# Opening of a four-layer graph network kernel: zero products while x arrives, a different order of x W, and nine small loads issued later

## The chip, the cores and the metric

One core of a Trainium2 chip. The metric is the device time of one execution in microseconds (us). Every kernel is timed in several rounds beside the kernel before, on the same chip; I quote the median of its runs and, in brackets, the lowest and the highest. One run of each kernel was recorded by the hardware profiler. Its "span", from first to last instruction, is some 1.8 us shorter than the timed figure of the same execution.

Engines: PE is TensorE (PEld its weight loads), DVE is VectorE, ACT is ScalarE, SP is SyncE. "ACTq" marks the issue of a load by ScalarE.

## The reference, cut to what matters

x is 4096 x 128, adj is 4096 x 4096 in fp32 (67 MB), read again by every layer. Each layer is followed by a residual and a layer norm. Only the first layer matters here:

```python
def _L0_gnn_ref(h, node_adj, edge_adj, W, a):        # both adjacencies are adj
    hw = h @ W
    pos = (node_adj > 0); neg = (node_adj < 0)
    h_plus = pos @ hw;    h_minus = neg @ hw
    a1, a2 = a[:F_OUT], a[F_OUT:]
    e_plus  = leaky_relu((h_plus @ a1 + h_minus @ a2)[:, 0], ALPHA)
    e_minus = ...
    scores = where(edge_adj > 0, e_plus[None, :], NEG_INF)
    scores = where(edge_adj < 0, e_minus[None, :], scores)
    attn = softmax(scores, axis=1)
    return attn * edge_adj @ hw
# [...] layers 1 to 3: Chebyshev convolution, four-head attention, GraphSAGE mean
```

The kernel uses that adj holds no negative entry (it checks this, and has another path if it fails). Then `h_plus @ a1` is `pos @ (h @ (W a1))`. So two columns u = x (W a) per node are enough for e, and x W with u appended is one product of 130 columns.

## The kernel before

adj arrives in blocks of 512 x 512 (1 MB each), eight for each of eight rounds. ScalarE issues the loads of x^T (eight pieces) and, right behind them, nine loads of small tensors that only later layers use:

```python
    for g in range(NB):
        nc.scalar.dma_start(xT[:, g * IB:(g + 1) * IB], xT_in[:, g * IB:(g + 1) * IB])
    B1A = load_const(b1a, [P, HH], "B1A")
    # [...] B1B, W2, ATS, ATD, B2R: loaded by ScalarE in the same way
    nc.scalar.dma_start(W2S[:, 0:F], w2T)
    nc.scalar.dma_start(W3[:, 0, :], w3n)
    nc.scalar.dma_start(W3[:, 1, :], w3s)

    def later_constants(psum, name):                # "the setup work"
        # [...] 8 small copies from ATS and ATD into att; a product of W2 and att
        nc.vector.tensor_tensor(W3[:, 1, :], W3[:, 1, :], ident, ALU.add)      # L118
        # [...] the mean of W3 by a product, subtracted from W3
```

The opening of the first layer, x W for 32 tiles of 128 nodes, then rounds over the blocks:

```python
            for g in range(NB):
                tb = slice(g * TB, (g + 1) * TB)
                for half in range(2):
                    # [...] pn <- two products of an x tile with WA = [W, W a]      (TensorE)
                    nc.vector.tensor_copy(u[:, two, :], pn[:, :, F:F + 2])        # L320
                    nc.scalar.copy(hw[:, two, :], pn[:, :, 0:F])                  # L321
                split3(both[:, tb, :], 0, u[:, tb, 0])      # u as three bf16 parts: 5 VectorE ops per 4 tiles
            later_constants(ps_mm, "pmm")

            for i in range(NB):                        # rounds
                # [...] for each of 8 blocks: pos = mask(a) on VectorE, sums of u over it on TensorE,
                #       a scan for negative entries on ScalarE, products of known blocks with hw
                parts = l0w.tile([P, IB], F32, name="parts")
                nc.scalar.copy(parts, pe)
                sums = columns(parts)                  # the round's column sums, L340
                # [...] e, exp(e), and hw scaled by it, on VectorE and ScalarE
```

The framework that builds the kernel orders each engine's instructions by itself. An instruction whose inputs look ready can move forward past others, unless it is pinned (`keep_in_program_order`) or depends on late data.

Of the kernel before, what the change touches and what calls it, by code (L numbers as in the profile page):

```python
# [11 lines left out]
F32 = mybir.dt.float32  # L12
BF16 = mybir.dt.bfloat16
I32 = mybir.dt.int32
AF = mybir.ActivationFunctionType
ALU = mybir.AluOpType
# [3 lines left out]
P = 128  # L20
IB = 512
TB = IB // P
# [11 lines left out]
def adj_resnorm_d4(ctx: ExitStack, tc: tile.TileContext, x_in, xT_in, adj, adjT, w0g, w0gT, a0, w1a, b1a,  # L34
# [7 lines left out]
    nc = tc.nc  # L42
# [13 lines left out]
    def load_const(src, shape, name):  # L56
        t = const.tile(shape, F32, name=name)
        nc.scalar.dma_start(t, src)
        return t
# [5 lines left out]
    W0 = load_const(w0g, [P, F], "W0")  # L65
    for g in range(NB):
        nc.scalar.dma_start(xT[:, g * IB:(g + 1) * IB], xT_in[:, g * IB:(g + 1) * IB])
    B1A = load_const(b1a, [P, HH], "B1A")
    B1B = load_const(b1b, [P, 1], "B1B")
    W2 = load_const(w2, [P, F], "W2")  # L70
    ATS = load_const(att_src.rearrange("o h f -> (h f) o"), [P, 1], "ATS")
    ATD = load_const(att_dst.rearrange("o h f -> (h f) o"), [P, 1], "ATD")
    B2R = load_const(b2.to_broadcast([P, F]), [P, F], "B2R")

    W2S = const.tile([P, F + H], F32, name="W2S")
    nc.scalar.dma_start(W2S[:, 0:F], w2T)
    W3 = const.tile([P, 2, F], F32, name="W3")
    nc.scalar.dma_start(W3[:, 0, :], w3n)
    nc.scalar.dma_start(W3[:, 1, :], w3s)

    ident = const.tile([P, P], F32, name="ident")
    make_identity(nc, ident)
# [10 lines left out]
    WD = const.tile([P, 96], F32, name="WD")  # L93
    selD = const.tile([96, H, P], BF16, name="selD")

    def later_constants(psum, name):

        with tc.tile_pool(name="setup", bufs=1) as pool:
            att = pool.tile([P, 2, H], F32, name="att")
            nc.vector.memset(att, 0.0)  # L100
            for h in range(H):
                hp = slice(h * FO, (h + 1) * FO)
                nc.vector.tensor_copy(att[hp, 0, h:h + 1], ATS[hp, :])
                nc.vector.tensor_copy(att[hp, 1, h:h + 1], ATD[hp, :])

            nc.vector.memset(WD, 0.0)
            pw = psum.tile([P, 2, H], F32, name=name)
            nc.tensor.matmul(pw, W2, att.rearrange("p s h -> p (s h)"), start=True, stop=True)
            nc.vector.tensor_copy(W2S[:, F:F + H], pw[:, 0, :])
            for part in range(3):  # L110
                nc.vector.tensor_copy(WD[:, 32 * part:32 * part + H], pw[:, 1, :])

            rows = pool.tile([96, H], F32, name="rows")
            nc.vector.tensor_reduce(rows, ident[0:96, :].rearrange("p (q c) -> p c q", q=4)[:, 0:H, 0:3], AX.X, ALU.add)
            nc.vector.tensor_copy(selD, rows[:, :, None].to_broadcast([96, H, P]))


            nc.vector.tensor_tensor(W3[:, 1, :], W3[:, 1, :], ident, ALU.add)  # L118
            mean = pool.tile([P, P], F32, name="mean")
            nc.vector.memset(mean, 1.0 / F)  # L120
            pw = psum.tile([P, 2 * F], F32, name=name)
            nc.tensor.matmul(pw, mean, W3.rearrange("p s f -> p (s f)"), start=True, stop=True)
            nc.vector.tensor_sub(W3.rearrange("p s f -> p (s f)"), W3.rearrange("p s f -> p (s f)"), pw)

    def chunk(pool, src, ib, c, name="chunk"):

        t = pool.tile([P, TB, IB], F32, name=name)
        nc.sync.dma_start(t, src[ib, c])
        return t
# [133 lines left out]
    def layer0(ld, ps_acc, ps_tr, ps_mm):  # L263
# [9 lines left out]
        with tc.tile_pool(name="l0", bufs=1) as l0, tc.tile_pool(name="l0w", bufs=2) as l0w, \  # L273
# [25 lines left out]
            def split3(dst, col, v):  # L299

                for part in range(3):
                    nc.vector.tensor_copy(dst[:, :, col + part], v)
                    if part < 2:
                        nc.vector.tensor_sub(v, v, dst[:, :, col + part])


            WA = l0.tile([P, F + 2], F32, name="WA")
            pw = ps_mm.tile([P, 2], F32, name="pmm")
            nc.tensor.matmul(pw, W0T, A0, start=True, stop=True)
            nc.vector.tensor_copy(WA[:, 0:F], W0)  # L310
            nc.vector.tensor_copy(WA[:, F:F + 2], pw)
            for g in range(NB):
                tb = slice(g * TB, (g + 1) * TB)
                for half in range(2):
                    two = slice(g * TB + 2 * half, g * TB + 2 * half + 2)
                    pn = ps_mm.tile([P, 2, F + 2], F32, name="pmm")
                    for k in range(2):
                        t = g * TB + 2 * half + k
                        nc.tensor.matmul(pn[:, k, :], xT[:, t * P:(t + 1) * P], WA, start=True, stop=True)
                    nc.vector.tensor_copy(u[:, two, :], pn[:, :, F:F + 2])  # L320
                    nc.scalar.copy(hw[:, two, :], pn[:, :, 0:F])  # L321
                split3(both[:, tb, :], 0, u[:, tb, 0])
            later_constants(ps_mm, "pmm")

            def masks(a):
                pos = l0w.tile([P, TB, IB], BF16, name="pos", bufs=4)
                nc.vector.tensor_scalar(pos, a, 0.0, None, op0=ALU.is_gt)
                return pos

            def edge_sums(pe, pos, j, wgt, first, last):  # L330

# [11 lines left out]
            def product(p, j, a, first, last):  # L343
                for k in range(TB):
                    nc.tensor.matmul(p, hw[:, j * TB + k, :], a[:, k, :], start=first and k == 0,  # L345
                                     stop=last and k == TB - 1)
# [24 lines left out]
            for i in range(NB):  # L371
# [6 lines left out]
                for n, j in enumerate(order):  # L378
                    if i < j <= i + 2:
                        a = chunk(l0k, adjT, i, j, f"keep{j - i}")  # L380
                        kept[i].append((j, a))
                    else:
                        a = chunk(ld, adjT, i, j)
                    own = a
                    pos = masks(a)
                    edge_sums(pe, pos, j, both, n == 0, n == NB - 1)
                    junk = l0w.tile([P, TB, IB], BF16, name="junk", bufs=1)
                    nc.scalar.activation(junk, a, AF.Relu, scale=-1.0, accum_out=bad[:, i * NB + n:i * NB + n + 1])
                    if n == 1 and rest:
                        diagonal(*rest)  # L390
                        if i >= 3:
                            above(i - 3, kept.pop(i - 3))
                    if j <= i and p is None and n > 0:
                        p = ps_acc.tile([P, IB], F32, name="pacc")
                    if j < i:
                        known.append((j, a))
                    while n > 0 and known:
                        j, a = known.pop(0)
                        product(p, j, a, j == 0, False)
                if i == 4:  # L400
                    tc.keep_in_program_order(nc.sync.dma_start(x, x_in.rearrange("(t p) f -> p t f", p=P)))
                parts = l0w.tile([P, IB], F32, name="parts")
                nc.scalar.copy(parts, pe)
# [621 lines left out]
```

## Time and profile before

| | kernel before |
|---|---|
| time before the prediction | 2262.8 us (2258.33 to 2266.13, 3 runs) |
| the execution that was profiled | 2259.04 us, span 2257.2 us |
| TensorE busy | 2134.4 us, 95% of the span |
| from 90 us on | TensorE nearly full |
| column sums of rounds 0, 1, 2 | 47.04, 65.53, 90.16 us |
| first product of the second layer | 348.0 us |

I use the last two rows as milestones throughout: they tell how far the kernel has come without waiting for the end.

A line of a timeline gives start, duration, engine, source line, operation, output and input with shapes; in brackets how long the engine stood idle before it and what ended that.

### The profile page before, as it was taken

The page shows a single profiled execution, that of the slowest core. Times are in us where ns is not written, and L with a number is a line of the kernel's source. Part 1 is how long each engine was busy: PE and PEld are TensorE (multiplying, and loading weights), DVE is VectorE, ACT ScalarE, POOL GpSimd, SP SyncE. Part 2 cuts the span into 40 slices and gives each one's busy share as a digit, 9 for nine tenths or more (in the row PEclk, how much of TensorE's full clock was granted, in tenths as well). Part 3 has the DMA queues.
Part 4 walks back from the last instruction along what each step waited for, and adds up shares of the span by engine and source line. Part 5 has one row for each costly group of instructions (what it writes and reads, how often), then busy time and mean ns, then how long its engine had stood idle before and what let it go on. Part 6 is the DMA issues. An engine that isn't in the chain of part 4 may idle for free. (4 is left out here: it accounts for less than half of the span.)

```text
span 2257.2 us, 22860 instructions
## 1 busy us (share of the span) xinstructions
PE 2134.4 (95%) x8560; PEld 847.2 (38%) x8560; DVE 1174.2 (52%) x1828; ACT 565.6 (25%) x1032; POOL 853.8 (38%) x539
## 2 busy tenths in 40 slices
PE   5899999999999999999999999968999899999997
PEld 3333444444444444444443333312222222323334
DVE  5544462000011100000025777779999999999995
ACT  5765200000000000000032322334343433332213
POOL 0000000000000000000004667679999899989990
PEclk8899999999999999999999999989999999999999
DMA  8886658888776676778766556614666566545545
GB/s 315 339 322 223 224 170 275 300 302 301 267 260 240 228 267 237 264 272 278 265 238 225 205 205 223 220 58 152 230 239 241 205 228 251 214 146 205 184 171 169
DMA packets 87144, 528.17 MB, mean 234 GB/s; under 512 B 9328, under 2 KB 15472, under 8 KB 25712
## 3 DMA queue, kind: packets, MB, share of 16 engines
q1 hardware_dynamic: 78992, 521.31, 65.6%
q10 hardware_dynamic: 8032, 5.31, 0.7%
q8 instruction: 69, 1.13, 0.2%
q14 instruction: 51, 0.42, 0.1%
HBM read 524.49 MB, written 2.10 MB: 233 GB/s over the span
## 5 line engine op out<-in xcount | busy, mean ns | idle before, releaser
L715 DVE SCALAR_TENSOR_TENSOR tau<-D,es,a 128x1024 f32<-128x1024 f32 (+1 forms) x640 | 646.3, 1058 | 60.2 <-ACT a L687 33.8
L721 POOL TENSOR_TENSOR tau<-tau,chunk 128x1024 f32<-128x1024 f32 x192 | 455.8, 2374 | 14.4 <-DVE tau L715 13.7
L621 POOL TENSOR_TENSOR x<-x,B2R 128x512 f32<-128x512 f32 x8 | 10.2, 1274 | 1172.6 <-PE px L135 1172.6
L737 PE MATMUL num<-tau,hc 128*32 128x512 f32 x2048 | 324.5, 615 | 12.9 <-POOL tau L721 6.0
L737 PE MATMUL den<-tau,cs 128*32 128x512 f32 x2048 | 331.5, 603 | 4.4 <-DVE tau L715 3.0
L813 PE MATMUL pp<-chunk,xT 128*128 128x512 f32 (+1 forms) x488 | 231.6, 604 | 0.9 <-ACT D L703 0.9
L687 ACT ACTIVATE a<-chunk 128x1024 f32<-128x1024 f32 x160 | 164.3, 1027 | 246.1 <-DVE tau L719 209.1
L513 PE MATMUL pacc<-chunk,t 128*128 128x512 f32 x512 | 223.5, 592 | 0.0
L513 PE MATMUL pacc<-chunk,v 128*128 128x512 f32 x512 | 222.5, 592 | 0.0
L513 PE MATMUL pacc<-chunk,x 128*128 128x512 f32 x512 | 221.9, 592 | 0.0
L720 POOL TENSOR_TENSOR tau<-tau,chunk 128x320 f32<-128x320 f32 x192 | 167.0, 870 | 140.4 <-DVE tau L715 78.7
L937 PE MATMUL pp<-chunk,w 128*128 128x512 f32 x448 | 203.6, 598 | 1.5 <-DVE oT L597 0.8
L345 PE MATMUL pacc<-chunk,hw 128*128 128x512 f32 x408 | 196.1, 621 | 2.3 <-DVE hw L410 2.3
L719 DVE TENSOR_TENSOR tau<-tau,a 128x704 f32<-128x704 f32 x192 | 168.5, 877 | 0.0
L727 POOL TENSOR_TENSOR tau<-tau,chunk 128x1024 f32<-128x1024 f32 x64 | 151.8, 2372 | 1.1
L737 PEld LDWEIGHTS den<-tau,cs 128*32 128x32 f32 x2048 | 78.9, 111 | 179.5 <-issue 102.8
L513 PEld LDWEIGHTS pacc<-chunk,v 128*128 128x128 f32 x512 | 97.2, 190 | 122.0 <-issue 122.0
L737 PEld LDWEIGHTS num<-tau,hc 128*32 128x32 f32 x2048 | 60.6, 110 | 218.5 <-issue 115.6
L513 PEld LDWEIGHTS pacc<-chunk,x 128*128 128x128 f32 x512 | 96.4, 190 | 116.7 <-issue 116.7
L513 PEld LDWEIGHTS pacc<-chunk,t 128*128 128x128 f32 x512 | 96.1, 190 | 115.3 <-issue 115.3
L813 PEld LDWEIGHTS pp<-chunk,xT 128*128 128x128 f32 x488 | 85.7, 189 | 130.3 <-issue 127.6
L560 DVE COPY w<-ptr 128x512 f32<-128x512 f32 x8 | 5.5, 691 | 241.5 <-PE ptr L135 241.5
(212 smaller groups left out, 1665.4 us busy)
## 6 DMA issues: line engine op xcount, KB each, us to landing
chunk<-in_adjT SPq DMA_DIRECT2D x386, 1024.0 KB, 4.8
chunk<-in_adj SPq DMA_DIRECT2D x80, 1024.0 KB, 5.0
chunk<-in_adj SPq DMA_DIRECT2D x32, 512.0 KB, 4.8
keep<-in_adjT SPq DMA_DIRECT2D x13, 1024.0 KB, 7.2
xT<-in_xT ACTq DMA_DIRECT2D x8, 256.0 KB, 6.2
out<-o ACTq DMA_DIRECT2D x7, 256.0 KB, 2.3
W1A<-in_w1a ACTq DMA_DIRECT2D x1, 384.0 KB, 5.9
W1B<-in_w1b ACTq DMA_DIRECT2D x1, 384.0 KB, 6.7
```

The lines of the kernel that those rows point to most:

```text
L345: nc.tensor.matmul(p, hw[:, j * TB + k, :], a[:, k, :], start=first and k == 0, stop=last and k == TB - 1)
L513: nc.tensor.matmul(p, stationary(c * TB + k), a[:, k, :], start=n == 0 and k == 0, stop=n == NB - 1 and k == TB - 1)
L621: nc.gpsimd.tensor_tensor(x[:, tb, :], x[:, tb, :], B2R[:, None, :].to_broadcast([P, TB, F]), ALU.add)
L687: nc.scalar.activation(ap, a, AF.Copy, accum_out=deg[:, nt, self.mp:self.mp + 1])
L715: nc.vector.scalar_tensor_tensor(flat(tau[:, q:q + n]), flat(self.D[:, q:q + n]), es[:, nt, head:head + 1], ap, op0=ALU.max, op1=ALU.mult)
L719: nc.vector.tensor_tensor(t2[:, 0:OWN], t[:, 0:OWN], ap[:, 0:OWN], ALU.mult)
L720: nc.gpsimd.tensor_tensor(t2[:, OWN:WB], t[:, OWN:WB], a[:, OWN:WB], ALU.mult)
L721: nc.gpsimd.tensor_tensor(t2[:, WB:2 * WB], t[:, WB:2 * WB], a, ALU.mult)
L727: nc.gpsimd.tensor_tensor(tau2[:, 2:4, :], tau[:, 2:4, :], rep(a, 2), ALU.mult)
L737: nc.tensor.matmul(acc[32 * q:32 * q + 32, :], weights(nt, head, is_den), r[:, q, :], start=nt == 0, stop=nt == NT - 1)
L813: nc.tensor.matmul(p, y[:, c * TB + k, :], a[:, k, lo:lo + n], start=c == blocks[0] and k == 0, stop=end)
L937: nc.tensor.matmul(p, w[:, c * TB + k, :], a[:, k, :], start=c == 0 and k == 0, stop=c == NB - 1 and k == TB - 1)
```

## The change

Its intent: keep TensorE awake while x arrives (28 products of zeros), take x W out of ScalarE's hands, do the split of u in two large pieces, and load the small inputs only when the opening is over.

```diff
-    B1A = load_const(b1a, [P, HH], "B1A")
-    # [...] B1B, W2, ATS, ATD, B2R, and the loads of W2S and W3
+    def later_inputs():
+        for t, src in ((B1A, b1a), (B1B, b1b), (W2, w2), (ATS, ...), (ATD, ...), (B2R, ...), (W2S[:, 0:F], w2T),
+                       (W3[:, 0, :], w3n), (W3[:, 1, :], w3s)):
+            tc.keep_in_program_order(nc.scalar.dma_start(t, src))
# [...] in later_constants: the copies from ATS and ATD and the add to W3 become pinned
+            idle = ps_tr.tile([P, IB], F32, name="ptr")
+            zeros = xp.rearrange("p t c -> p (t c)")
+            for n in range(28):
+                nc.tensor.matmul(idle, zeros[:, 0:P], zeros[:, 0:IB], start=True, stop=True)
-            WA = l0.tile([P, F + 2], F32, name="WA")
+            WA = l0.tile([P, F + 4], F32, name="WA")
+            nc.vector.memset(WA[:, F + 2:F + 4], 0.0)
# [...]
-                    nc.scalar.copy(hw[:, two, :], pn[:, :, 0:F])
-                split3(both[:, tb, :], 0, u[:, tb, 0])
-            later_constants(ps_mm, "pmm")
+                    nc.vector.tensor_copy(hw[:, two, :], pn[:, :, 0:F])
+                if g % 2:
+                    a = chunk(ld, adjT, 0, 3 + g // 2)
+                    begun.append((a, masks(a, True)))          # a mask after every 8 tiles of x W, pinned
+                if g % 4 == 3:
+                    half = slice((g - 3) * TB, (g + 1) * TB)
+                    split3(both[:, half, :], 0, u[:, half, 0]) # 16 tiles at once
# [...] in the rounds
+                if i == 2:
+                    later_inputs()
                 if i == 4:
+                    later_constants(ps_mm, "pmm")
```

More of the change, by code (lines that the diff above doesn't have):

```diff
@@ L67, in adj_resnorm_d4 @@
         nc.scalar.dma_start(xT[:, g * IB:(g + 1) * IB], xT_in[:, g * IB:(g + 1) * IB])
-    B1A = load_const(b1a, [P, HH], "B1A")
-    B1B = load_const(b1b, [P, 1], "B1B")
-    W2 = load_const(w2, [P, F], "W2")
-    ATS = load_const(att_src.rearrange("o h f -> (h f) o"), [P, 1], "ATS")
-    ATD = load_const(att_dst.rearrange("o h f -> (h f) o"), [P, 1], "ATD")
-    B2R = load_const(b2.to_broadcast([P, F]), [P, F], "B2R")
+    B1A, B1B, W2 = [const.tile(shape, F32, name=name) for name, shape in (("B1A", [P, HH]), ("B1B", [P, 1]), ("W2", [P, F]))]
+    ATS, ATD, B2R = [const.tile(shape, F32, name=name) for name, shape in (("ATS", [P, 1]), ("ATD", [P, 1]), ("B2R", [P, F]))]
     W2S = const.tile([P, F + H], F32, name="W2S")
-    nc.scalar.dma_start(W2S[:, 0:F], w2T)
     W3 = const.tile([P, 2, F], F32, name="W3")
-    nc.scalar.dma_start(W3[:, 0, :], w3n)
-    nc.scalar.dma_start(W3[:, 1, :], w3s)
     ident = const.tile([P, P], F32, name="ident")
@@ L94, in adj_resnorm_d4 @@
     selD = const.tile([96, H, P], BF16, name="selD")
+    def later_inputs():
+        for t, src in ((B1A, b1a), (B1B, b1b), (W2, w2), (ATS, att_src.rearrange("o h f -> (h f) o")),
+                       (ATD, att_dst.rearrange("o h f -> (h f) o")), (B2R, b2.to_broadcast([P, F])), (W2S[:, 0:F], w2T),
+                       (W3[:, 0, :], w3n), (W3[:, 1, :], w3s)):
+            tc.keep_in_program_order(nc.scalar.dma_start(t, src))
     def later_constants(psum, name):
@@ L102, in later_constants @@
                 hp = slice(h * FO, (h + 1) * FO)
-                nc.vector.tensor_copy(att[hp, 0, h:h + 1], ATS[hp, :])
-                nc.vector.tensor_copy(att[hp, 1, h:h + 1], ATD[hp, :])
+                for s, v in enumerate((ATS, ATD)):
+                    tc.keep_in_program_order(nc.vector.tensor_copy(att[hp, s, h:h + 1], v[hp, :]))
             nc.vector.memset(WD, 0.0)
@@ L115, in later_constants @@
             nc.vector.tensor_copy(selD, rows[:, :, None].to_broadcast([96, H, P]))
-            nc.vector.tensor_tensor(W3[:, 1, :], W3[:, 1, :], ident, ALU.add)
+            tc.keep_in_program_order(nc.vector.tensor_tensor(W3[:, 1, :], W3[:, 1, :], ident, ALU.add))
             mean = pool.tile([P, P], F32, name="mean")
@@ L304, in split3, with masks @@
                         nc.vector.tensor_sub(v, v, dst[:, :, col + part])
-            WA = l0.tile([P, F + 2], F32, name="WA")
+            def masks(a, pinned=False):
+                pos = l0w.tile([P, TB, IB], BF16, name="pos", bufs=4)
+                r = nc.vector.tensor_scalar(pos, a, 0.0, None, op0=ALU.is_gt)
+                if pinned:
+                    tc.keep_in_program_order(r)
+                return pos
+            idle = ps_tr.tile([P, IB], F32, name="ptr")
[4 more added lines that the diff above has]
+            nc.vector.memset(WA[:, F + 2:F + 4], 0.0)
             pw = ps_mm.tile([P, 2], F32, name="pmm")
@@ L311, in layer0 @@
             nc.vector.tensor_copy(WA[:, F:F + 2], pw)
+            begun = []
             for g in range(NB):
-                tb = slice(g * TB, (g + 1) * TB)
                 for half in range(2):
                     two = slice(g * TB + 2 * half, g * TB + 2 * half + 2)
-                    pn = ps_mm.tile([P, 2, F + 2], F32, name="pmm")
+                    pn = ps_mm.tile([P, 2, F + 4], F32, name="pmm")
                     for k in range(2):
@@ L320, in layer0 @@
                     nc.vector.tensor_copy(u[:, two, :], pn[:, :, F:F + 2])
-                    nc.scalar.copy(hw[:, two, :], pn[:, :, 0:F])
-                split3(both[:, tb, :], 0, u[:, tb, 0])
-            later_constants(ps_mm, "pmm")
-            def masks(a):
-                pos = l0w.tile([P, TB, IB], BF16, name="pos", bufs=4)
-                nc.vector.tensor_scalar(pos, a, 0.0, None, op0=ALU.is_gt)
-                return pos
+                    nc.vector.tensor_copy(hw[:, two, :], pn[:, :, 0:F])
[5 more added lines that the diff above has]
+                    split3(both[:, half, :], 0, u[:, half, 0])
             def edge_sums(pe, pos, j, wgt, first, last):
@@ L381, in layer0 @@
                         kept[i].append((j, a))
-                    else:
+                    elif not begun:
                         a = chunk(ld, adjT, i, j)
                     own = a
-                    pos = masks(a)
+                    if begun:
+                        a, pos = begun.pop(0)
+                    else:
+                        pos = masks(a)
                     edge_sums(pe, pos, j, both, n == 0, n == NB - 1)
```

## The prediction

> **What bounds the kernel now.** I read the page's busy slices, then busy time by stretch, then the opening in order of time.
>
> The page's slices (tenths busy, 56 us each):
> ```profile
> PE   5899999999999999999999999968999899999997
> ```
> TensorE is full from the third slice on. The only large hole that this change can touch is in the first two slices, so I cut those finely.
>
> Busy time by stretch (start:end, length, busy us and count of PE, PEld, DVE, ACT, POOL, granted clock, DMA share, GB/s):
> ```profile
> 0.00:40.00 40.00, 15.74 (x70) 12.65 (x70) 17.20 (x73) 16.72 (x26) 0.70 (x6) 0.92 0.95 366
> 40.00:50.00 10.00, 6.97 (x52) 3.80 (x52) 7.90 (x26) 8.03 (x13) 0.00 (x0) 0.84 0.17 61
> 50.00:90.00 40.00, 33.61 (x120) 13.06 (x120) 19.65 (x32) 32.34 (x37) 0.00 (x0) 0.82 0.99 408
> 90.00:348.00 258.00, 254.11 (x918) 108.67 (x918) 132.18 (x291) 96.13 (x117) 0.00 (x0) 0.99 0.67 236
> 348.00:1110.00 762.00, 760.58 (x1928) 346.51 (x1928) 54.01 (x108) 38.10 (x61) 0.00 (x0) 1.00 0.78 267
> ```
> Three regimes. To 40 us the DMA engines are 95% busy: the opening is bound by the arrival of adjacency blocks (1 MB each, eight per round) and x. From 40 to 50 they are nearly idle (61 GB/s) although data is still wanted: buffers were not freed. From 50 to 90 they are full again while TensorE catches up. From 90 to 1110 us TensorE is busy 1014.69 of 1020 us, so what is saved before 90 us moves everything later forward and should be kept.
>
> The timeline shows why buffers were late:
> ```profile
> 2.15 8.61 ACTq L67 DMA_DIRECT2D xT<-in_xT  x8
> ...
> 10.01 2.10 PE L319 MATMUL pmm<-WA,xT 128*128 128x130 f32 x8 [0.39 <-DVE WA L310]
> ...
> 18.91 1.28 ACT L321 ACT_TABLE_LOAD   x1 [18.91 <-DMA W<-in_w]
> 20.20 0.65 ACT L321 COPY hw<-pmm 128x256 f32<-128x256 f32 x2
> 20.63 1.80 PEld L319 LDWEIGHTS pmm<-WA,xT 128*128 128x128 f32 x8 [8.82 <-ACT hw L321]
> 20.63 2.10 PE L319 MATMUL pmm<-WA,xT 128*128 128x130 f32 x8 [8.52 <-ACT hw L321]
> ```
> ScalarE issues loads until 18.9 us: nine of them, from 11.1 us on, are small inputs of later layers. Only then does it copy x W out of PSUM, for which TensorE has waited 8.5 us. Afterwards those copies alternate with its 2.1 us sign checks (1.92 plus 0.20) of each block, so the x W stage lasts from 10.0 to 42.6 us. The first round's column sums start at 47.04 us, the second's at 65.53, the third's at 90.16.
>
> **What the Trainium skill says.** "TensorE: Matmul & The Clock Gate", "What's actually happening": the array's clock is halved by default and is released after some 3.4 us of activity. The trace agrees: weight loads of the x W stage have a median of 335 ns and a minimum of 186, the second half at 40.9 us and later. Its caveat that the clock records are unreliable applies: they grant 1.00 at 10 to 12 us, where a load took 337 ns.
> "DMA: Bandwidth & Descriptors", "Issuing engines are not separate DMA queues": loads from ScalarE and SyncE share the same engines, and a second issuer saves issue time only. The trace agrees: with both issuing, the share is 0.95 and no more than 0.99 later. Moving loads frees ScalarE but makes little bandwidth.
> "VectorE: DVE Perf Modes", "Why PSUM operands drop a tier": fp32 out of PSUM runs at one element a cycle. The trace has 408 ns for 128x256 (an add out of PSUM, L123), which I use for the moved copies; ScalarE took 373.
>
> **The change part by part.**
> 1. Zero products: 28 on bf16 zeros, starting after the second memset (2.0 us), beside loads that last until 9.1 us. They are 512 columns; the trace's 1024 column-passes in 592 ns include drain, and four successive fp32 records at full clock step 1.98/4 = 0.495 us for twice the columns, so about 0.23 us warm. With eight at 0.45 and twenty at 0.23 (estimate) they end near 10 us. Cost nil. Gain: weight loads at 188 instead of 335 ns in the x W stage, 64 x 0.147 = 9.4 us of that engine, but overlapped and partly hidden behind VectorE and DMA.
> 2. 132 columns instead of 130: nothing. The minimum of 275 ns is no slow path; four memset columns are idle work.
> 3. Copies: 16 x 0.373 = 6.0 us leave ScalarE, 16 x 0.408 = 6.5 us come to VectorE. Splits: 8 x 5 x 0.172 = 6.9 us become 2 x 5 x 0.18 = 1.8. VectorE in round 0 stays near 16 x (0.41 + 0.16) + 8 x 1.22 + 1.8 = 21 us. From 10.7 us on that gives the eighth mask at about 32 us.
> 4. Loads later: ScalarE is free at 10.8 us, table load until 12.1, then eight checks at 2.1 = 17 us, paced by arrivals (8 MB + 2.1 MB of x at 0.41 MB/us after a slow first 10 us, so the eighth block at about 29 us). The order view of the new program has the ninth check ahead of the column sums' copy: sums near 35 us instead of 47.
> 5. So buffers free by 34 us and the DMA hole of 40 to 50 us should close: (1 - 0.17) x 10 = **8.3 us**. Without it the second round's last block lands near 51 us, checked at 53, and its sums begin at 54 to 55 instead of 65.53: **10 to 11 us**. This includes about 1 us of small-input traffic (0.4 MB) taken out of the way.
> 6. Given back. The nine loads are issued by ScalarE at the end of round 2, ahead of the copy of its sums: 9 x 0.44 = 4 us, of which that engine had 2.08 idle there. The order view also puts five copies from those inputs on VectorE ahead of round 2's e chain; they wait for loads that took 6.6 and 7.5 us to land before. VectorE had 7.58 us idle there, so I count 2 us lost. The two small setup products (0.39 + 0.70 us) move into the full regime: 1 us more.
>
> Sum: -11 for the hole and earlier checks, +2 for the late inputs, +1 for setup products, -1 for a warmer start: -9 us. 2262.8 - 9 = 2253.8, say **2254 us** (0.4%).
>
> **The rivals.** (a) The DMA bound hides it all: the blocks arrive no faster, and 0 to 40 us is already at 366 GB/s. For it: the 0.95. Against: ten nearly idle microseconds follow. Pure arrival gives exactly the 8.3 us, about 2254.
> (b) The late inputs become the new wait: ScalarE issuing into a full DMA queue and VectorE waiting for att_src at the third round's end, as it waited 1.83 us for it before. TensorE would stand for 5 to 8 us, the clock would fall, and the gain shrinks to 2 to 5 us: 2258 to 2261.
> (c) The clock as the main lever: the trace has it at 0.50 at 48 to 54 and 66 to 74 us too. If the earlier flow of products also keeps TensorE awake there, each stretch of about 6 busy us at half rate returns 3 us more: 2246 to 2248. Against: the zeros end at 10 us, and rounds 0 and 1 contain few products, 0.4 us of column sums per 2.5 us block.
> (d) VectorE becomes the bound of the x W stage, masks and copies in one order: 21 us against ScalarE's old 32; still a gain.
>
> **Range and chances.** (b) and (c) bracket the middle: 2246 to 2261. The three runs before spread over 8 us, which adds about 2 below. I take 2244 to 2261. Over 2% is 45 us; TensorE's idle time in the first 90 us is 90 - 15.74 - 6.97 - 33.61 = 33.7 us, so even its whole removal falls short: 0.02. Slower by 2% would need a stall that no part contains, since the orders differ only in the first layer: 0.01.
>
> **What would show it.** Right: ScalarE's table load at about 11 us; x W finished before 30 us with weight loads near 190 ns; no stretch at low GB/s around 40 us; column sums of rounds 0, 1, 2 at about 35, 54 and 79 us; TensorE full thereafter and the second layer's first product near 339 us instead of 348. Wrong: sums of round 1 still past 60 us; VectorE waiting several us for ATS or ATD ahead of round 2's e; TensorE idle or at 0.50 after 80 us; or later stages longer by themselves.

## More of the kernel before

```profile
23.82 0.29 DVE L118 TENSOR_TENSOR W<-W,ident 128x128 f32<-128x128 f32 x1 [2.31 <-DMA W<-in_w3s]
...
25.35 0.65 ACT L321 COPY hw<-pmm 128x256 f32<-128x256 f32 x2 [2.60 <-DVE u L320]
...
47.04 1.64 PE L340 MATMUL ptr<-sel,parts 128*128 128x2 f32 x8
65.53 1.87 PE L340 MATMUL ptr<-sel,parts 128*128 128x2 f32 x8 [2.74 <-ACT parts L403]
90.16 1.05 PE L340 MATMUL ptr<-sel,parts 128*128 128x2 f32 x8 [0.69 <-ACT parts L403]
```

VectorE adds the identity to W3, setup work for the last layer, in the middle of the opening, because the scheduler had moved it forward; it waited 2.31 us for the load of W3. The u copies stand behind it on VectorE, so ScalarE, which empties the same PSUM tile after them, stood 2.60 us too.

## The result and the profile after

The changed kernel takes 2249.08 us (2248.86 to 2249.32, 4 runs), the kernel before in the same rounds 2263.94 us (2258.33 to 2266.13, 4 runs). The ratio is 0.9938, interval 0.9919 to 0.9957. Ratios here are the mean time of one kernel's fast runs over that of the other's in the same rounds, so they are not quite the ratio of the medians. By the medians the gain is 14.9 us. The two profiled executions differ less: 2259.04 to 2249.32 us, spans 2257.2 to 2247.5, 9.7 us.

Busy time by stretch of the changed kernel, the same cuts as in the prediction (start:end, length, then busy us and count of PE, PEld, DVE, ACT, POOL, granted clock, DMA share, GB/s):

```profile
0.00:40.00 40.00, 26.39 (x143) 15.31 (x144) 23.93 (x74) 23.86 (x25) 0.70 (x6) 0.84 0.97 387
40.00:50.00 10.00, 10.00 (x32) 3.66 (x31) 6.48 (x9) 6.34 (x8) 0.00 (x0) 0.79 1.01 421
50.00:90.00 40.00, 29.27 (x116) 12.23 (x115) 21.64 (x44) 30.66 (x36) 0.00 (x0) 0.77 0.91 346
90.00:348.00 258.00, 257.41 (x929) 112.14 (x928) 130.87 (x310) 89.32 (x109) 0.00 (x0) 1.00 0.69 237
```

The hole in the transfers at 40 to 50 us (61 GB/s before) is gone: 421 GB/s. From 90 us on TensorE is full to within 0.6 us, where before it stood 3.9 us of that stretch.

The opening of the changed kernel in order of time:

```profile
2.06 8.48 PE L317 MATMUL ptr<-xp 128*128 128x512 bf16 x28 [2.06 <-DVE xp L292]
...
10.73 1.28 ACT L403 ACT_TABLE_LOAD   x1 [10.73 <-DMA xT<-in_xT]
...
10.91 1.17 PE L332 MATMUL pmm<-WA,xT 128*128 128x132 f32 x8 [0.25 <-DVE WA L324]
...
35.43 1.87 PE L352 MATMUL ptr<-sel,parts 128*128 128x2 f32 x8 [0.62 <-ACT parts L421]
55.26 1.87 PE L352 MATMUL ptr<-sel,parts 128*128 128x2 f32 x8 [3.21 <-ACT parts L421]
82.01 1.87 PE L352 MATMUL ptr<-sel,parts 128*128 128x2 f32 x8 [2.41 <-ACT parts L421]
```

Eight records of x W (the trace shows each fp32 product as two records) take 1.17 us, where six of the eight such groups took 2.10 before; ScalarE's table load comes at 10.73 in place of 18.91 us, and the last copy of x W starts at 24.0 us in place of 42.6. The column sums of rounds 0, 1 and 2 come 11.6, 10.3 and 8.2 us earlier. The second layer's first product starts at 338.9 us in place of 348.0: 9.1 us, and from there on nothing more is gained.

So part of the 11.6 us is given back by the end of round 2. The timeline of the changed kernel there:

```profile
76.69 0.72 ACTq L94 DMA_DIRECT2D ATS<-in_att_src  x1
...
80.99 0.34 ACTq L94 DMA_DIRECT2D W<-in_w3s  x1
81.37 0.59 ACT L421 COPY parts<-pden 128x512 f32<-128x512 f32 x1 [4.01 <-DMA W2S<-in_w2T]
81.53 0.14 DVE L104 COPY att<-ATS 32x1 f32<-32x1 f32 x1 [4.73 <-DMA ATS<-in_att_src]
...
88.40 5.48 PE L357 MATMUL pacc<-chunk,hw 128*128 128x512 f32 x8
```

ScalarE issues the nine loads between the round's last scan and the copy of its sums, and stands 4.01 us; VectorE stands 4.73 us for att_src. The first product of the next round starts 6.4 us after the column sums; before it was 3.4 us. Whether that costs anything at the end is a question for the experiments.

### The profile page after: what moved, and what is told of

The parts are those of the page before. It is cut to its first block, busy times and chain, and to the rows that moved or that the text cites. A ratio compares the mean times of both kernels' runs of the same rounds, so it can differ in the third digit from the quotient of the medians.

```text
span 2247.5 us, 22889 instructions
## 1 busy us (share of the span) xinstructions
PE 2138.4 (95%) x8588; PEld 848.3 (38%) x8588; DVE 1174.6 (52%) x1815; ACT 561.9 (25%) x1016; POOL 854.4 (38%) x539
## 5 line engine op out<-in xcount | busy, mean ns | idle before, releaser
L739 POOL TENSOR_TENSOR tau<-tau,chunk 128x1024 f32<-128x1024 f32 x192 | 456.0, 2375 | 14.4 <-DVE tau L733 13.6
```

The lines of the kernel that those rows point to most:

```text
L739: nc.gpsimd.tensor_tensor(t2[:, WB:2 * WB], t[:, WB:2 * WB], a, ALU.mult)
```

## The experiments

Two questions. Why do the timed medians differ by 14.9 us where the profiles differ by 9.7? And which part of the change carries the gain?

**Theory A**: ScalarE, held by nine issues, is late with its table load and its copies; that and the order of the opening is the gain, as the prediction has it. **Theory B**: what held the opening is VectorE's wait for a small load. **Rivals**: the zeros and the clock; the columns; who copies; and, for what was given back, the row of issues at the end of round 2.

All milestones below are from each kernel's one profile; times are of its unprofiled and profiled runs together. The kernel before had medians of 2264.83 (2255.95 to 2266.59), 2264.83 (2258.72 to 2267.82) and 2263.19 us (2255.61 to 2268.78) beside the three batches, 11 runs each. The batches ran on three different chips (e1, e4, e5, e7; then e0, e2, e3, e8; then e6, e9, e10, e11), and the intervals of the ratios are some 0.003 to 0.004 wide, 7 to 10 us. So a difference of one or two us between rows of different batches is not shown by the times.

| label | time, us | ratio to before (95%) | column sums of rounds 0, 1, 2, us | second layer starts, us |
|---|---|---|---|---|
| kernel before | 2263.94 | | 47.04, 65.53, 90.16 | 348.0 |
| e0_before_again | 2262.38 (2258.15, 2266.61) | 0.9992 (0.9964 to 1.0021) | 53.80, 72.86, 97.65 | 355.6 |
| e5_only_zeros | 2264.98 (2258.17 to 2266.80) | 1.0007 (0.9992 to 1.0022) | 46.78, 64.54, 89.29 | 347.4 |
| e7_only_late_inputs | 2256.55 (2254.66 to 2258.28) | 0.9972 (0.9958 to 0.9986) | 43.23, 62.12, 89.09 | 345.0 |
| e9_setup_later | 2251.59 (2250.14 to 2253.17) | 0.9955 (0.9933 to 0.9976) | 43.69, 62.66, 87.42 | 343.6 |
| e3_early_inputs | 2253.89 (2252.41 to 2255.89) | 0.9957 (0.9941 to 0.9972) | 39.72, 59.57, 84.39 | 342.1 |
| e2_act_copies | 2250.12 (2247.68 to 2251.45) | 0.9936 (0.9920 to 0.9951) | 39.99, 58.30, 83.74 | 340.6 |
| e8_awake | 2250.77 (2248.22 to 2253.50) | 0.9944 (0.9928 to 0.9960) | 41.72, 65.58, 86.17 | 343.6 |
| e4_inputs_sync | 2248.95 (2246.67 to 2250.02) | 0.9934 (0.9920 to 0.9949) | 36.02, 56.42, 81.51 | 342.5 |
| e10_inputs_spread | 2249.08 (2248.01 to 2250.33) | 0.9942 (0.9921 to 0.9963) | 35.72, 55.80, 80.71 | 340.0 |
| e1_no_zeros | 2249.14 (2248.49 to 2250.64) | 0.9939 (0.9925 to 0.9953) | 33.99, 55.39, 83.11 | 339.5 |
| e6_cols_130 | 2249.17 (2247.59 to 2250.39) | 0.9942 (0.9921 to 0.9964) | 35.57, 55.08, 82.34 | 339.0 |
| changed kernel | 2249.08 (2248.86 to 2249.32) | 0.9938 (0.9919 to 0.9957) | 35.43, 55.26, 82.01 | 338.9 |
| e11_after_again | 2249.44 (2247.47 to 2249.86) | 0.9943 (0.9922 to 0.9964) | 35.78, 55.25, 81.69 | 339.1 |

### e0_before_again: the kernel before, unchanged

> The kernel before once more, for a second profile. Its timed runs lie between 2256 and 2266.6 us while its first profile came from a run of 2259.0. Theory: a slow run of it loses its 6 us in the opening (before 100 us), where arrival, checks and clock interact, and not in the later layers; then a profile of 2264 us or more shows the second layer's first product at 353 us or later instead of 348.0. Rival: the spread comes from the attention stage: then 348 us again and the difference after 1100 us.

Its profiled execution was a long one, 2266.61 us, span 2264.7. That was luck: it shows what the first profile could not. The second layer starts at 355.6 us, 7.6 later than in the first profile, and the end is 7.5 us later: all of the difference arises in the opening. Its timeline:

```profile
32.00 0.29 DVE L118 TENSOR_TENSOR W<-W,ident 128x128 f32<-128x128 f32 x1 [10.47 <-DMA W<-in_w3s]
...
33.54 0.65 ACT L321 COPY hw<-pmm 128x256 f32<-128x256 f32 x2 [10.85 <-DVE u L320]
...
33.96 2.10 PE L319 MATMUL pmm<-WA,xT 128*128 128x130 f32 x8 [11.30 <-ACT hw L321]
```

The same add, and 10.47 us of wait in place of 2.31. Behind it stand the u copies, behind them ScalarE for 10.85 us, behind it TensorE for 11.30 us. Read from the bottom, each line names the one above as its releaser; the top one names a load. The view of that load (who waited, and the time from issue to landing) in this execution:

```profile
  DVE W L118: 10.5, 1
...
DMA to landing us min/median/max: 13.6/13.6/13.6
```

and in the first profile of the same kernel:

```profile
DMA to landing us min/median/max: 5.5/5.5/5.5
```

The issue is at 18.3 and 18.4 us, alike; the landing differs by 8.1 us, VectorE's wait by 8.2, the end by 7.5. Theory B has its mechanism. It is still one pair of profiles, so e9 tests it.

### e9_setup_later: the kernel before, with the waiting taken away

```diff
-            later_constants(ps_mm, "pmm")          # after x W
# [...] in round 4:
+                    later_constants(ps_mm, "pmm")
# [...] inside it: att's memset and copies pinned, and the add made to depend on late data
-            nc.vector.tensor_tensor(W3[:, 1, :], W3[:, 1, :], ident, ALU.add)
+            one = pool.tile([P, 1], F32, name="one")
+            nc.vector.tensor_scalar(one, W2S[:, F:F + 1], 0.0, 1.0, op0=ALU.mult, op1=ALU.add)
+            nc.vector.scalar_tensor_tensor(W3[:, 1, :], ident, one, W3[:, 1, :], op0=ALU.mult, op1=ALU.add)
```

The nine loads stay where they were. A pin alone does not hold the add back (in e3, below, the pinned add runs at 29.51 us, in the opening), so it now multiplies the identity by a 1 that is computed from the result of the setup product.

> The kernel before, with its nine small loads still issued by ScalarE in the opening, but with the setup work that reads them (the att copies and their product, the identity added to W3, the mean product) moved to the end of round 4 of the first layer, tied there by data, so that VectorE waits for no small load while x W is made. What it tells apart: why the kernel before is 8 us slower in most executions than in its fastest, and what of the gain of the late inputs belongs to VectorE's wait and what to ScalarE's issues. Theory (VectorE's wait for the W3 load, 2.3 us in one profile and 10.5 us in a slower one, is the whole spread and over half of the gain): 2255 to 2259, all runs within 4 us of each other, ScalarE's table load still near 19 us, x W done near 31, sums of round 0 at 43 to 46. Rival (ScalarE being late with its table load is what counts, and the landing of the small loads costs the opening through the queue itself): 2261 to 2265, runs spread over 7 us or more as before.

Measured: 2251.59 us, 11.6 below the kernel before of the same rounds, and all six runs within 3.0 us where the kernel before spread over 13. That is better than the 2255 to 2259 that theory B expected, and far from the rival. ScalarE's table load and the load of W3, in this execution:

```profile
18.97 1.28 ACT L323 ACT_TABLE_LOAD   x1 [18.97 <-DMA ATS<-in_att_src]
...
43.69 1.86 PE L341 MATMUL ptr<-sel,parts 128*128 128x2 f32 x8
```

```profile
DMA to landing us min/median/max: 13.5/13.5/13.5
```

ScalarE is as late as before, and W3 took 13.5 us to land, as in the long execution of e0; but nobody waits for it, and the sums come at 43.69 us, not 53.80. Theory B is shown: with the waits for small loads gone the spread falls from 13 to 3.0 us. e9 moves the setup products as well, but they are not what it gains by: from the last copy of x W to round 0's sums it takes 4.4 us in the first profile (42.61 to 47.04) and 4.9 in e9 (38.79 to 43.69), so the gain lies before that copy, where the waits were. Of the gain e9 has 11.6 of 13.7 us by the medians of these rounds; by the second layer's start it is 12.0 of 16.7 us against the long execution of e0 and 4.4 of 9.1 us against the short one that the first profile caught. The rest is not in e9: its stretch of 40 to 50 us, where the DMA share was 0.17 before and 1.01 after, reads

```profile
40.00:50.00 10.00, 7.69 (x36) 3.88 (x37) 7.35 (x20) 7.60 (x9) 0.00 (x0) 0.56 0.44 158
```

More than half of the hole is left (0.44), as its opening is still 4.7 us behind the changed kernel's.

### e7_only_late_inputs: the small loads later, nothing else

```diff
# the kernel before, with later_inputs() at the end of round 2 and later_constants() at the end of round 4,
# and with the pins of the changed kernel; no zeros, 130 columns, copies on ScalarE, split every 4 tiles
```

> The kernel before with nothing but the small inputs (and setup products) moved later. Theory (both ScalarE's issues and its copies between checks delay the x W stage): ScalarE's table load at 11 us, round 0's sums at about 40 us, half of the gain there, and some 5 us lost at the end of round 2: time 2257 to 2262 us. Rival (the issues alone made the hole): round 0's sums at 36 us, time 2249 to 2252 us.

Measured: 2256.55 us, 8.3 below the kernel before, with a spread of 3.6 us; the theory's 2257 to 2262 and 40 us missed, and the rival's figures too. In the opening of this kernel both waits are away, VectorE's and ScalarE's:

```profile
11.43 1.28 ACT L321 ACT_TABLE_LOAD   x1 [11.43 <-DMA xT<-in_xT]
...
25.42 2.10 PE L319 MATMUL pmm<-WA,xT 128*128 128x130 f32 x8
...
36.62 1.24 PE L319 MATMUL pmm<-WA,xT 128*128 128x130 f32 x4
...
43.23 1.86 PE L338 MATMUL ptr<-sel,parts 128*128 128x2 f32 x8
```

ScalarE is ready 7.5 us earlier than in e9, yet round 0's sums come at 43.23 against 43.69 us. So theory A's first half falls for the old order: ScalarE's early arrival brought half a microsecond. Something else paces x W there: the products of the last x tiles still run at 36.62 us. The early groups wait for an hw copy behind a 1.91 us scan and a u copy behind a 1.23 us mask (TensorE stands 1.20 and 1.49 us at 16.45 and 19.18 us); from 25 us on they follow a block's sums, which wait 0.75 to 1.16 us for the split of u.

A rival stands beside the order. All of e7's x W runs at the slow pace, 2.10 us for eight records, where e9 has

```profile
25.61 1.16 PE L321 MATMUL pmm<-WA,xT 128*128 128x130 f32 x8 [0.80 <-ACT hw L323]
```

and three more groups near it (1.16, 1.37, 1.16). The seven groups after the first take 10.7 us in e9 and at 2.10 us each would take 14.7 in e7: 4 us (estimate) of the 7 that e7 loses of ScalarE's lead. No run has the old order, an early ScalarE and a fast TensorE together, so how much of the loss is the order and how much the pace of TensorE stays open.

### e2_act_copies: the changed kernel with the copies back on ScalarE

```diff
-                    nc.vector.tensor_copy(hw[:, two, :], pn[:, :, 0:F])
+                    nc.scalar.copy(hw[:, two, :], pn[:, :, 0:F])
```

> The changed kernel with the x W copies back on ScalarE. Theory: late inputs alone gave 8.3 us, so the copies on VectorE (with the masks placed between them and the splits by 16) are worth the other 5 to 7 us; ScalarE's copies wait behind checks of 2.1 us, round 0's sums come at 39 to 43 us instead of 35.4, time 2252 to 2257 us. Rival (the splits and pinned masks made the difference, not who copies): 2249 to 2251 us.

Measured: 2250.12 us. The theory (2252 to 2257) missed, its rival held. Round 0's sums move from 35.4 to 40.0 us, but the second layer starts only 1.7 us later and the end, by the medians, 0.7 to 1.0 us, which is within the noise: later rounds absorb the rest. Against e7 (43.23, 345.0) this kernel has the new order of masks and the split by 16 tiles, with zeros and columns that turn out to be worth nothing: order and split together bring 3.2 us at round 0 and 4.4 us at the second layer's start. (TensorE's pace is not quite the same in the two: three of e2's eight groups of x W take 2.13 us, the others less.)

### e3_early_inputs: the changed kernel with the small loads early again

```diff
+    later_inputs()                                  # right after the loads of x
# [...]
-                if i == 2:
-                    later_inputs()
```

> The changed kernel with the small inputs issued by ScalarE at the start as before, setup products still late. Theory: the table load is back at about 19 us, the checks run late, round 0's sums move from 35.4 to 38 to 42 us, but nothing is lost at the end of round 2: time 2250 to 2256 us. Rival (only who copies matters): 2247 to 2249 us.

Measured: 2253.89 us, 4 to 5 above the changed kernel, inside the theory's range. ScalarE's table load is back at 19.00 us. The copies into att were meant for round 4 but the scheduler put them in the opening, and VectorE waited there:

```profile
18.39 0.14 DVE L106 COPY att<-ATS 32x1 f32<-32x1 f32 x1 [4.46 <-DMA ATS<-in_att_src]
```

It is the same kind of wait, at another instruction, so this run does not tell ScalarE's lateness from VectorE's wait. That the pins of the changed kernel don't hold these copies back is worth knowing: they stand behind a memset that isn't pinned and which floats to the start (1.96 us here). Where it is pinned too, they stay behind it: at 137.6 us in e9, 200.2 in e10 and 202.9 in e4.

### e5_only_zeros and e1_no_zeros: the zero products alone, and all but them

```diff
# e5: the kernel before, plus:            e1: the changed kernel, minus:
    idle = ps_tr.tile([P, IB], F32, name="ptr")
    zeros = xp.rearrange("p t c -> p (t c)")
    for n in range(28):
        nc.tensor.matmul(idle, zeros[:, 0:P], zeros[:, 0:IB], start=True, stop=True)
```

> The kernel before with nothing but the 28 zero products. Theory (ScalarE's issues until 18.9 us and its checks hold the x W stage, not the clock): round 0's sums within 2 us of 47.0, time 2259 to 2264 us. Rival (the clock is the main lever): 2254 us or less. Side question: if the zeros pin the clock, the runs of this kernel spread by less than 2 us.

> The changed kernel (2249.1 us) without the 28 zero products. Theory (arrival and ScalarE order make the gain, the warm clock is hidden behind them): weight loads of the x W stage go back to about 335 ns, but round 0's sums stay within 2 us of 35.4 us, round 1's near 55 to 57; time 2249 to 2252 us. Rival (the clock is the main lever): round 0's sums after 40 us, time 2254 us or more. Side question: the changed kernel's four runs lie within 0.5 us, the one before spreads over 8 us; if the zeros pin the clock in the opening, this kernel's runs spread by 3 us or more.

Measured: 2264.98 us (before 2264.83) and 2249.14 us (changed 2249.08). The zeros are worth nothing, alone or with the rest. But they say less of the clock than was hoped. In e1 the weight loads of x W did not go back to 335 ns: their median is 190 and their mean 222, against 189 with zeros, as only the first records are slow. In e5 the zeros end at 10.0 us, TensorE stands 6.06 us for ScalarE until 20.37, and every group of x W takes 2.00 to 2.10 us. So neither run shows what a fast TensorE through x W is worth in the old order. Without zeros in the changed kernel round 0's sums even come earlier, at 33.99 us: the zeros end at 10.5 us and hold back the product of W0T, which starts at 9.07 us without them and at 10.38 with them. That lead is gone by round 1 (55.39). The kernel before with zeros keeps its spread of 8.6 us; and in the long execution of e0 the last four groups of x W ran fast (1.16 us), so a slow TensorE does not explain why that one was long.

### e6_cols_130: the changed kernel with 130 columns

```diff
-            WA = l0.tile([P, F + 4], F32, name="WA")
-            nc.vector.memset(WA[:, F + 2:F + 4], 0.0)
+            WA = l0.tile([P, F + 2], F32, name="WA")
# [...] and pn likewise
```

> The changed kernel with products x W of 130 columns in place of 132 (one part undone). Theory: nothing, 2248.5 to 2250 and within 0.7 us of the changed kernel of the same rounds; x W stage within 0.5 us. Rival (132 columns make the products or their weight loads quicker, by reading or writing PSUM in whole pieces): the weight loads of x W above 195 ns in place of 190 or products longer by over 5%, sums of round 0 later by 1 us or more.

Measured: 2249.17 us, the changed kernel of the same rounds 2249.44; the milestones agree to 0.7 us. Eight records of 130 columns take 1.16 us, of 132 columns 1.17. The columns are worth nothing.

### e8_awake: more zero products, in rounds 0 to 2

```diff
+                    if i < 2:
+                        awake(6)                      # 6 zero products after each block's sums
# [...]
+                if i < 3:
+                    awake(8)                          # 8 after the column sums
```

> The changed kernel with more zero products: 6 behind each block's column sums in rounds 0 and 1, 8 behind the sums of rounds 0 to 2, to keep the clock up where it fell to 0.50. Theory: round 1 and round 2 then start warm (the eight records at 39.68 us took 5.94 instead of 3.70, those at 59.51 and 63.77 took 6.21 instead of 3.8, the sums 1.87 instead of 0.95 three times), worth 3 to 6 us: 2243 to 2246 us. Rival (those records wait for arrival or are hidden): 2248 to 2250 us, or slower if the extra products stand in the way.

Measured: 2250.77 us; the theory missed. The fillers did what they should to the clock: from 40 to 90 us it is granted in full (1.00, changed kernel 0.77 to 0.79), and the column sums take 0.95 to 1.05 us in place of 1.87. But they come later, at 41.72, 65.58 and 86.17 us, because pinned fillers stand ahead of real work (TensorE does not stand at all from 40 to 50 us). The start of the second layer is 4.7 us later; the end is 1.3 to 1.7 us later by the medians, which is within the noise between batches. This run says that the clock can't be bought in this way; it doesn't say what a warm clock would be worth if it came free, and no run here does.

### e4_inputs_sync and e10_inputs_spread: what the row of nine issues costs

```diff
# e4: issued by SyncE at the end of round 4, setup work at the end of round 6, att's memset pinned
-            tc.keep_in_program_order(nc.scalar.dma_start(t, src))
+            tc.keep_in_program_order(nc.sync.dma_start(t, src))
# e10: issued by ScalarE one by one, one after each block's scan in rounds 3 and 4; setup as in e4
+                    if i >= 3 and n > 1 and small_inputs:
+                        tc.keep_in_program_order(nc.scalar.dma_start(*small_inputs.pop(0)))
```

> The changed kernel with the nine small inputs issued by SyncE in round 4 and the setup products in round 6 (their first memset pinned as well). Theory (late inputs give back some 5 us at the end of round 2: ScalarE waits 4.0 us in its issues, VectorE 4.7 us for ATS): the step from round 1's sums to round 2's shrinks from 26.75 to 24 to 25 us, the first product follows the sums by 3.4 instead of 6.4 us, time 2243 to 2246 us. Rival (TensorE's backlog or DMA sets round 3's start anyway): 2248 to 2250 us.

> The changed kernel, with the nine small loads issued by ScalarE one by one, one after each tile's scan in rounds 3 and 4 in place of all nine in a row at the end of round 2, and with the setup work at the end of round 6. Theory (the changed kernel gives back about 5 us of wait at the end of round 2 to the nine issues in a row and to VectorE's copies, most of it hidden): sums of round 3 at 109.5 to 110.5 in place of 111.3, no first wait over 4 us at the end of round 2, and 2246 to 2248, 1 to 3 us under the changed kernel of the same rounds. Rival (the transfers of the first layer bind from round 3 on, and a wait taken from one place returns at the next, as when SyncE issued them): 2248 to 2250, no difference over 1 us.

Measured: 2248.95 and 2249.08 us; both theories missed, both rivals held. The wait is indeed away. The timeline of e10:

```profile
80.07 0.58 ACT L422 COPY parts<-pden 128x512 f32<-128x512 f32 x1 [2.07 <-PE pden L344]
...
84.15 3.78 PE L356 MATMUL pacc<-chunk,hw 128*128 128x512 f32 x4
...
177.34 0.40 PE L344 MATMUL pmm<-pos,xp 128*32 128x512 bf16 x4 [0.29 <-DVE pos L307]
...
179.15 3.70 PE L356 MATMUL pacc<-chunk,hw 128*128 128x512 f32 x8 [1.41 <-DVE hw L429]
```

The first product of round 3 starts at 84.15 in place of 88.40 us, a lead of 4.2 us over the changed kernel. Where it goes can be followed in the two timelines. The first eight records of the round take longer, 6.6 us until the next instruction starts against 5.4 (four of them 3.78 us, twice the 1.98 of four later ones), so that the next ones lead by 2.8 us (91.54 against 94.36). Then TensorE waits in e10 where the changed kernel does not: 0.33 us at 113 us, and 0.29 and 1.41 us at 177 to 179 us (e4: 1.78 us at 178.96). The last of these is a wait for the scaling of hw after round 5's column sums. These come at the same time in both kernels (174.81 and 174.74 us), but after them the changed kernel still has products of kept blocks to do, and e10 has done more of them before. At 183 us the lead is 0.4 us (183.33 against 183.75), and by then the changed kernel has done its two setup products (0.28 and 0.70 us), which e10 has only at 210 us. So e10 is 0.6 us behind by this count, and 1.1 at the second layer by the profile. The row of nine issues costs up to 4.2 us where it stands, and the time won by taking it away went into other waits. (e7 has the same row in the old order: from 0.5 us ahead of e9 at round 1's sums it falls 1.7 behind at round 2's and is 1.4 behind at the second layer. There the row may well cost something.)

### e11_after_again: the changed kernel, unchanged

> The changed kernel itself, unchanged, as control of the same rounds and for its spread. Theory (in the changed kernel nothing waits for a small load in the opening): 2248 to 2250.5, all runs within 3 us, sums of rounds 0, 1 and 2 within 1 us of 35.4, 55.3 and 82.0. Rival (the first four runs fell well by chance and the opening varies with the landings as before): a spread of 6 us or more.

Measured: 2249.44 us (2247.47 to 2249.86). The opening repeats to 0.4 us and the spread is 2.4 us. With the waits for small loads out of the opening, the landing times no longer reach the end.

### What stays open

The rest of the program, from the second layer's end on, took between 1154.1 us (e8; e9 1154.9) and 1159.4 us (e3) by the profiles; 1158.0 in the changed kernel, 1158.1 in the kernel before. e9's opening is 4.7 us behind the changed kernel's and its end only 2.1 to 2.5 us. No run here tells why, nor why the same load lands after 5.5 us in one execution and after 13.6 in another. So ends are compared to no better than some 2 to 3 us, and the finer steps are read from the milestones.

## Why the prediction was right or wrong

The range held, and 2254 was 4.9 us above what came. That it held is in part luck: its lower part stood there for (c), the clock, and 2 us for the spread, and (c) did not come. Point by point:

- **Step 1, zeros**: cost nil was right. The zeros end at 10.5 us, expected near 10; sixteen of them step 0.21 us, expected 0.23. The "warmer start" of 1 us was not right: x W's weight loads do take 186 to 190 ns, as expected, but e1, without zeros, has a median of 190 too and the same time. (In the kernel before, the fast loads were not a "second half" either: of the eight groups, those at 31.93 and 40.48 us were fast, those at 35.04 and 37.62 slow.)
- **Step 2, columns**: nothing, shown by e6. (The memset columns are two, not four.)
- **Step 3, copies and splits to VectorE**: VectorE does carry them (the eighth mask runs from 30.6 to 31.8 us, expected at about 32). The milestones of e9 and the changed kernel put the new order, the copies, the split and ScalarE's earlier start together at 4.7 us (343.6 to 338.9), of which the copies are 1.7 (e2).
- **Step 4, ScalarE free at 10.8 us, sums near 35**: both came (10.73, 35.43). But the reason does not carry it alone: with ScalarE free at 11.4 us and the old order, the sums stay at 43.23 us (e7). Order, split and copies had to change too (e2: 39.99), or TensorE had to be faster; e7 does not tell these apart.
- **Step 5, the hole closes and round 1's sums come at 54 to 55**: 421 GB/s and 55.26 us. As a measure the hole served: 8.3 us of it, 9.1 us gained at the second layer's start, and e9, with over half of the hole left, is 4.7 us behind. As a cause it did not: it shows that buffers came free late, not what held them. ScalarE was named; e9 shows VectorE's wait (4.4 of the 9.1 us), and e7 that freeing ScalarE was not enough. That -9 agrees so well with the profiles is therefore luck in part: the size came from the hole, and the prediction named one of its causes.
- **Step 6, given back**: 3 us were counted, 2 of them at the end of round 2. The lead shrinks from 11.6 us at round 0's sums to 8.2 at round 2's, which come at 82.01 us where the signs said 79. The setup products took 0.98 us in the full stretch, as counted (1 us). But e10 took the waits away and the end did not move, so the 2 us are not shown as a cost at the end.
- **The sum** of -9 us is what the profiles show at the second layer's start (9.1) and about what they show at the end (9.7).

**The step that failed by most is the last line of the sum**, "2262.8 - 9 = 2253.8". The -9 was worked out from a profile whose execution took 2259.04 us, and taken off a median that belongs mostly to other executions. From 2259.04 it gives 2250, 1 us off. Of the 39 timed runs of the kernel before, 9 were under 2260 us; the first profile had caught such a one. The prediction saw the spread of 8 us, called it 2 us of uncertainty, and did not ask what made it. The answer stood in the profile: VectorE's 2.31 us for W3, in line with TensorE and ScalarE behind it. That wait grows with the load's landing time, and the change takes it away whole. So a typical execution gains some 4 to 6 us more than the profiled one (medians of 2263.19 to 2264.83 against 2259.04).

Of the rivals, (a), pure arrival, gave the same 2254 and rested on the same hole; no run separates it from the main line. (b) came true in its mechanism (4.73 us for att_src) without its cost. (c) did not come: from 40 to 90 us the granted clock went from 0.82 to 0.77 by the records; e8 forced it up and came to the second layer 4.7 us later. (d) may well describe the x W stage, where VectorE was busy 11.24 of the 12.85 us from 11.60 to 24.45; but that stage was over at 24 us, so it cost nothing that shows.

Neither e4 nor e10 beats the changed kernel by more than the runs' spread, so it stays the best of those tried.

## What to carry to other kernels

Look in the opening for instructions of later stages that wait for a load. Here the scheduler moved one forward because nothing held it, and everything on its engine stood behind it; move the use, not only the load, and tie it by data where a pin is not enough. When a kernel's runs spread, profile a slow and a fast run and find the instruction where they part before taking any gain off the median.

The smallest fix here was e9 (11.6 us): the loads may stay early if nobody asks for them early. The Trainium skill says the same in "DMA: Bandwidth & Descriptors", "Rules for kernel authors": issue a transfer early, compute, and wait late. The trace agrees: the load that took 13.6 us cost 10.47 us of VectorE in e0, and one that took 13.5 us cost nothing in e9.

## What the Trainium skill lacked or had wrong

- "DMA: Bandwidth & Descriptors", "Latency and other measured facts", gives a fixed cost of a transfer of about 2 us and an access latency that rises at high load, but not how far the landing of a small load varies between executions when the engines are full. Here the same 64 KB load, issued at the same time into the same stream, took 5.5, 13.6 and 13.5 us in three executions.
- "TensorE: Matmul & The Clock Gate", "Seeing it yourself", warns that clock records have been unreliable, and this holds: e7's record grants 1.00 for the first 40 us while eight x W records take 2.10 us, where fast ones take 1.16. The page does not say how to tell beforehand whether work that keeps the array awake will pay; here zeros brought the mean weight load of x W from 222 to 189 ns and were worth 0 us (e1), and fillers in rounds 0 to 2 put the second layer off by 4.7 us (e8).
- "ScalarE: Activation LUTs", "What ACT_TABLE_LOAD costs", states some 1283 ns for the load and some 1380 ns more of drain for a switch. The load agrees (1.28 us); no drain is seen at this first load: in the kernel before it starts at 18.91 us and the copy follows at 20.20.
- No page says that a scheduler may move an instruction of a later stage ahead of its neighbours and so put a wait into an opening; the runs show 2.31 to 10.47 us for one such instruction.
